# A decoder layer on one core: the expert's down projection written as two 64-token products per chunk

## The chip, the core and the metric

The kernel runs on one core of a Trainium2 chip. The core has five engines with a queue each: PE (TensorE, matrix products; the loading of its weights is listed apart as PEld), DVE (VectorE), ACT (ScalarE), POOL (GpSimd) and SP (SyncE, which here only issues transfers). PE reads its operands from SBUF and writes into PSUM[...]; DVE and ACT copy results out of it. The metric is the time of one execution on the device in microseconds, as the median of several runs. The profile is of one further execution.

## The reference, cut to what matters

One decoder layer with the normalisation after each part: causal self attention of 16 heads, linear cross attention to a context, then a mixture of experts with 8 experts of which each token uses two. There are 8 sequences of 112 tokens, so 896 tokens of 512 numbers. The change concerns the experts:

```python
gate_up = einsum('th,ehj->etj', h, gate_up_proj) + gate_up_proj_bias
gate = minimum(gate_up[..., ::2], 7);  up = clip(gate_up[..., 1::2], -7, 7)
act = (up + 1.0) * gate * sigmoid(1.702 * gate)
expert_out = einsum('eti,eih->eth', act, down_proj) + down_proj_bias
out = einsum('te,eth->th', scores, expert_out)
```

The inner size of an expert is 512, as is the size of a token. Everything is f32.

## The kernel before, in words

The layer is one stream of work. Up to about 755 us it does the two attentions, the routing, and the first product of the experts. From there on the experts' part has the core alone. Tokens have been sorted by expert into blocks of 128 in the DRAM tensor `store`, and the part is a loop over `STEPS` = 21 blocks, whatever the routing was.

For one block `s`:

- `fetch_tokens` (POOL, L944) brings the block's 128 tokens, `fetch_weights` (SP, L917 and L925) brings three matrices of 512x512 of the block's expert, `wg`, `wu` and `wd`, 1 MB each. They lie in 12 slabs of SBUF, three for each of the four blocks that can be ahead.
- `start` turns the tokens with four transposes on PE (`bT_ps`, L975), and ACT copies the result to SBUF (`bT`, L979).
- `project(s, st, k)` makes the gate (k = 0) and the up part (k = 1): four products over the chunks `c` of 128 of the contraction (L1054), summed in one PSUM bank, and then bias, limits and product on DVE and the sigmoid on ACT.
- `transposed_block` turns the activated block, again with four transposes on PE (`aT_ps`, L975) and a copy on ACT (`aT`, L979).
- `down(s, st)` is the down projection: four products over the chunks (L1080), with the stationary operand `aT[:, c, :]`, which is 128 rows of the contraction by 128 tokens, and the moving operand `wd[:, c, :]`, 128 rows by 512 columns. The result is 128 tokens by 512 in one bank, `yps`. ACT copies it to SBUF as `y` (L1091), and POOL adds it to the rows of `total` with an indirect DMA (L1094). In the last block, `finish` adds one more product into the same bank (L1198) and DVE reads it (L1199).

A product in f32 appears in the profile as two passes, each with its own weight load. So the four products of one `down` are eight matmul records and eight weight loads.

The order on PE, DVE, ACT and SP is that of the program text (`tc.manual_schedule`). In the loop over `s`, PE runs: gate product of block `s`, transposes of the activated block `s-1`, transposes of the tokens of block `s+1`, up product of block `s`, down product of block `s-1`. In the first blocks a few small products of the routing of the last tokens stand between these: `sTps` (L588, 8 columns of weights), `lps` (L515), `cps` (L540, L541) and `dbps` (L594, 8 rows of contraction). In the last ones `keys` (L1178) stands ahead of the down product. After the loop has reached its end, the last tokens are normalised (`close_steps`) and written to the output by POOL (`write`, L1129).

## Time and profile before

| | us |
|---|---|
| median of three runs (lowest, highest) | 1000.46 (999.9, 1000.54) |
| the profiled execution | 998.96 |
| its span, first to last instruction | 997.4 |
| PE busy | 963.8 |
| PE weight loads busy | 505.1 |
| DVE busy | 462.5 |
| ACT busy | 244.7 |
| POOL busy | 185.2 |
| matmuls of the down projection, 168 records, busy | 75.9 |
| mean granted clock of TensorE | 0.993 of full speed |

A matmul record lasts longer than its place in the stream[...]. So the mean of a record (595 ns for the down projection) isn't its cost; the distance from one start to the next is, or the busy time of the group divided by its count. In the chain of work that ended last the pieces are laid end to end, so that a piece's length is the time it took from the path.

### The profile page before, as it was taken

To read this page: it belongs to the slowest core of one execution; us is meant where nothing else is said; L and a number is where in the kernel's file an instruction comes from. 1 tells how busy PE (TensorE), PEld (TensorE's weight loads), DVE (VectorE), ACT (ScalarE), POOL (GpSimd) and SP (SyncE) were. 2 spreads that over 40 slices of the span, in tenths; PEclk is the share of its full clock that TensorE was granted. 3 is DMA by queue.
4 is the path that set the end of the run, shared out by engine and by line. 5 is a ranking of instruction groups with operands and counts; after the bars stand their busy time and mean duration, and the time that the engine had idled before them with its cause. 6 is when DMAs were issued, how large, how long until landed. Compare 5 with 4: busy or idle time off the path is not lost.

```text
span 997.4 us, 9419 instructions
## 1 busy us (share of the span) xinstructions
PE 963.8 (97%) x3271; PEld 505.1 (51%) x3271; DVE 462.5 (46%) x1036; ACT 244.7 (25%) x430; POOL 185.2 (19%) x235
## 2 busy tenths in 40 slices
PE   7998999999999999999999999999899999999994
PEld 3455544566446555654555455555454444444442
DVE  1356511154213542574414566567775533334384
ACT  1132311133103311322222222333124211121132
POOL 3133200033001414020002222211101212111132
PEclk9999999999999999999999999999999999999998
DMA  9990004111010001131001010110489997692333
GB/s 337 367 342 26 1 1 168 43 42 44 0 46 39 1 1 43 43 104 31 1 0 31 9 50 36 53 63 32 151 346 370 328 391 218 202 344 46 95 86 82
DMA packets 33839, 114.99 MB, mean 115 GB/s; under 512 B 3845, under 2 KB 8005, under 8 KB 26240
## 3 DMA queue, kind: packets, MB, share of 16 engines
q1 hardware_dynamic: 26784, 98.28, 26.9%
q0 software_dynamic: 6336, 15.75, 6.6%
q8 instruction: 26, 0.43, 0.2%
q10 hardware_dynamic: 672, 0.36, 0.1%
q14 instruction: 21, 0.17, 0.1%
HBM read 115.83 MB, written 29.01 MB: 145 GB/s over the span
## 4 chain that ended last, share of the span: by engine, by line
PE 86%; DVE 7%; issue 3%; ACT 1%; POOL 1%; DMA 1%; SPq 0%; POOLq 0%; DVEq 0%; ACTq 0%
PE gups L1054 13%; PE ops L237 10%; PE yps L1080 6%; PE vps L327 6%; PE zps L435 3%; PE xqps L870 2%; PE xgps L870 2%; PE sumps L812 2%; PE sps L387 2%; PE xops L237 2%; DVE z L843 1%; PE pps L427 1%; PE aT_ps L975 1%; PE bT_ps L975 1%; DVE p L412 1%
## 5 line engine op out<-in xcount | busy, mean ns | idle before, releaser
L1054 PE MATMUL gups<-slab,bT 128*128 128x512 f32 x336 | 151.5, 593 | 2.0 <-ACT bT L979 2.0
L1054 PEld LDWEIGHTS gups<-slab,bT 128*128 128x128 f32 x336 | 61.9, 190 | 71.4 <-issue 68.4
L237 PE MATMUL ops<-slab,zT 128*128 128x512 f32 x224 | 97.9, 592 | 0.0
L1062 DVE TENSOR_TENSOR gu<-gups,biases 128x512 f32<-128x512 f32 x42 | 29.0, 691 | 114.8 <-PE gups L1054 114.8
L1080 PE MATMUL yps<-slab,aT 128*128 128x512 f32 x168 | 75.9, 595 | 2.3 <-ACT aT L979 2.3
L237 PEld LDWEIGHTS ops<-slab,zT 128*128 128x128 f32 x224 | 42.0, 190 | 50.3 <-issue 49.5
L275 POOL TENSOR_TENSOR ws<-slab 128x256 f32<-128x256 f32 x16 | 11.8, 739 | 282.0 <-PE qk_5c L291 83.0
L327 PE MATMUL vps<-slab,x0T 128*112 128x512 f32 x128 | 58.6, 612 | 1.0 <-DVE x0T L187 0.8
L1094 POOL DMA_INDIRECT total<-y,nums x19 | 30.4, 1602 | 134.6 <-ACT y L1091 61.2
L1080 PEld LDWEIGHTS yps<-slab,aT 128*128 128x128 f32 x168 | 31.2, 190 | 40.6 <-issue 37.1
L244 DVE TENSOR_TENSOR xn<-xn,ops 128x512 f32<-128x512 f32 x28 | 19.2, 685 | 55.3 <-PE ops L237 55.2
L435 PEld LDWEIGHTS zps<-pT,v 112*128 112x128 f32 x256 | 33.5, 192 | 12.3 <-issue 11.2
L327 PEld LDWEIGHTS vps<-slab,x0T 128*112 128x112 f32 x128 | 22.8, 183 | 31.3 <-issue 29.7
L442 DVE COPY zT<-zps 128x448 f32<-128x448 f32 x32 | 20.0, 624 | 39.8 <-PE zps L435 39.8
L411 DVE TENSOR_REDUCE nm<-p 112x4 f32<-112x448 f32 x32 | 19.7, 616 | 30.9 <-POOL p L401 30.9
L435 PE MATMUL zps<-pT,v 112*128 112x112 f32 x256 | 33.4, 273 | 0.0
L1091 ACT COPY y<-yps 128x512 f32<-128x512 f32 x20 | 11.7, 584 | 87.8 <-issue 79.8
L237 PE MATMUL xops<-slab,gate 128*128 128x512 f32 x56 | 27.3, 632 | 3.8 <-DVE gate L845 2.6
L1066 ACT ACTIVATE sg<-gu 128x512 f32<-128x512 f32 x21 | 13.2, 630 | 71.2 <-DVE gu L1064 53.6
L565 POOL DMA_INDIRECT store<-xn,rows x14 | 13.9, 992 | 81.3 <-DVE count L627 52.5
L395 ACT ACTIVATE p<-sps 112x448 f32<-112x448 f32 x32 | 17.4, 544 | 45.6 <-PE sps L387 45.6
L387 PE MATMUL sps<-k,q 128*112 128x112 f32 x256 | 28.0, 262 | 0.0
(799 smaller groups left out, 1649.4 us busy)
## 6 DMA issues: line engine op xcount, KB each, us to landing
slab<-in_wg_dram SPq DMA_DIRECT2D x21, 1024.0 KB
slab<-in_wu_dram SPq DMA_DIRECT2D x21, 1024.0 KB
slab<-in_wd_dram SPq DMA_DIRECT2D x21, 1024.0 KB
store<-slab SPq DMA_DIRECT2D x8, 1806.0 KB
biases<-gubs SPq DMA_DIRECT2D x21, 512.0 KB
cT<-in_ctxT_dram SPq DMA_DIRECT2D x8, 750.0 KB
xblk<-store POOLq DMA_DIRECT2D x21, 258.0 KB, 7.4
slab<-in_wq_dram SPq DMA_DIRECT2D x4, 1024.0 KB
```

What stands on the lines that cost most here:

```text
L237: nc.tensor.matmul(ps, aT[:, c, t * P : (t + 1) * P], w[:, c, :], start=(c == 0), stop=(c == C - 1),)
L327: nc.tensor.matmul(ps[:S, :], xT[:, c, b * S : (b + 1) * S], w[:, c, :], start=(c == 0), stop=(c == C - 1),)
L387: nc.tensor.matmul(ps[:S, i * S : (i + 1) * S], qk["q"][:, rows], qk["k"][:, rows], start=True, stop=True,)
L435: nc.tensor.matmul(zps[:, i * S : (i + 1) * S], v[:, half * 4 + i, hl * DH : (hl + 1) * DH], pT[:, i * S : (i + 1) * S], start=True, stop= ...
L442: nc.vector.tensor_copy(zT[:, hl, half * HALF : (half + 1) * HALF], zps[:, :HALF])
L812: nc.tensor.matmul(sums[:, j, :], kf[:, sc, g * P : (g + 1) * P], vs[:, sc, g, :], start=(sc == 0), stop=(sc == NSC - 1),)
L870: nc.tensor.matmul(ps[:, :HALF], w[:, c, g * P : (g + 1) * P], xT[:, c, cols], start=(c == 0), stop=(c == C - 1),)
L975: nc.tensor.transpose(ps[:, c * P : (c + 1) * P], src[:, c * P : (c + 1) * P], ident)
L1054: nc.tensor.matmul(ps, st["bT"][:, c, :], st["w"][k][:, c, :], start=(c == 0), stop=(c == C - 1),)
L1062: nc.vector.tensor_add(a, ps, st["bias"][:, k * I : (k + 1) * I])
L1080: nc.tensor.matmul(ps, st["aT"][:, c, :], st["wd"][:, c, :], start=(c == 0), stop=(c == C - 1 and s < STEPS - 1),)
L1094: put = nc.gpsimd.indirect_dma_start(out=total, out_offset=bass.IndirectOffsetOnAxis(ap=st["num"], axis=0), in_=y, in_offset=None, compute ...
```

## The change

Each of the four products of `down` becomes two: one for the tokens 0 to 63, into partitions 0 to 63 of the bank, and one for the tokens 64 to 127, into partitions 64 to 127. Both have the same moving operand. The stationary operand of each is 64 columns wide, so the built program gives the first the tile of 128 rows by 64 columns of the array at column 0, and the second that at column 64. All other products of the loop keep the tile of 128 by 128. The order in `down` is, for each chunk: both passes of the first half, and then both passes of the second half. Nothing else is changed, and no other engine has an instruction more or less, or in another place.

```diff
         def down(s: int, st):
             ps = bank(f"yps_{s}", "aux")
             for c in range(C):
-                nc.tensor.matmul(
-                    ps,
-                    st["aT"][:, c, :],
-                    st["wd"][:, c, :],
-                    start=(c == 0),
-                    stop=(c == C - 1 and s < STEPS - 1),
-                )
+                for rows in (slice(0, P // 2), slice(P // 2, P)):
+                    nc.tensor.matmul(
+                        ps[rows],
+                        st["aT"][:, c, rows],
+                        st["wd"][:, c, :],
+                        start=(c == 0),
+                        stop=(c == C - 1 and s < STEPS - 1),
+                    )
```

## The prediction

> **What bounds the kernel now.** I read the first lines of the page, then the chain of work that ended last, since a busy share doesn't say whether an engine sets the end. The page's shares and its chain:

> ```profile
> PE 963.8 (97%) x3271; PEld 505.1 (51%) x3271; DVE 462.5 (46%) x1036; ACT 244.7 (25%) x430; POOL 185.2 (19%) x235
> ...
> PE 86%; DVE 7%; issue 3%; ACT 1%; POOL 1%; DMA 1%; SPq 0%; POOLq 0%; DVEq 0%; ACTq 0%
> ...
> L1080 PE MATMUL yps<-slab,aT 128*128 128x512 f32 x168 | 75.9, 595 | 2.3 <-ACT aT L979 2.3
> L1080 PEld LDWEIGHTS yps<-slab,aT 128*128 128x128 f32 x168 | 31.2, 190 | 40.6 <-issue 37.1
> ```

> PE is the bound, and the down projection has 75.9 us of it, with 2.3 us of waiting before it in the whole run. Then the same chain in order of time, from 755 us on. Columns: start, length (both us), engine and group, number of passes:

> ```profile
> 783.99 3.44 PE yps L1080 x8
> 787.42 0.32 PE sTps L588 x2
> 787.74 3.63 PE gups L1054 x8
> ...
> 795.67 1.05 PE dbps L594 x2
> 796.73 3.63 PE yps L1080 x8
> 800.36 3.43 PE gups L1054 x8
> ...
> 908.68 3.43 PE yps L1080 x8
> ...
> 942.43 0.22 PE keys L1178 x2
> ```

> From 755 to 965 us the chain holds PE alone, without a gap. A down projection is 3.43 us for 8 passes, so a pass of 512 columns costs 0.429 us. Whatever is added to PE there is added to the end.

> The groups that are longer than their work are the only places where the trace shows the array in another tile. `keys` and `sTps` are two passes of 128 columns each; `keys` takes 0.22, `sTps`, whose weights are 8 columns wide, takes 0.32, and the eight gate passes after it 3.63 where 3.43 is usual. `dbps` has 8 rows; it takes 1.05 where two passes are 0.86, and the group after it again 3.63. So going into another tile costs 0.10 (8 weight columns) to 0.19 us (128 columns), coming back 0.20. The weight loads in order of time say why:

> ```profile
> 786.40 0.19 PEld L1080 LDWEIGHTS yps<-slab,aT 128*128 128x128 f32 x1 [0.24 <-issue]
> 787.35 0.10 PEld L588 LDWEIGHTS sTps<-ident,sco 128*8 128x8 f32 x2 [0.76 <-DVE gu L1073]
> 787.66 0.30 PEld L1054 LDWEIGHTS gups<-slab,bT 128*128 128x128 f32 x2 [0.22 <-issue]
> ```

> Loads come every 0.43 us, each at the start of the pass before its own. The load for `sTps` comes 0.95 after its predecessor (0.43 + 0.52): it isn't made ahead. The same holds on the way back.

> [...] the first pass after a switch is recorded with 697 ns instead of 592, 105 more, and the difference between 0.19 and 0.10 is some 0.09 us for 120 columns.

> **The change, part by part.** It removes 8 passes per block and adds 16, each of 512 columns. The width of the weights isn't in the price of a pass: the 8-column passes of `sTps` still took 0.11 us each for 128 moving columns, as those of `keys` did. So by work alone PE has 16 × 0.429 = 6.86 us per block instead of 3.43. What saves it is only that the two halves run side by side; at best they come back to what one product does already. Nothing is there to gain from the shorter loads, as loads are hidden now (passes are 0.429 apart with loads of 0.19).

> *The order matters.* Call the halves A and B, and their passes 1 and 2. The stream is A1 A2 B1 B2 for each chunk. [...] So the pairs that overlap are A2 with B1, and B2 with the next chunk's A1. With l for the time that a 64-column load shows, 105 × 64/128 = 0.053 us (estimate from the recorded 697 − 592):

> - In this trace each load starts when the pass before its own starts, never sooner. Then B1's load begins with A2, and B1 runs l later. A1 at 0, A2 at 0.429, B1 at 0.482, B2 at 0.911, next A1 at 0.964. The last B2 starts at 3 × 0.964 + 0.911 = 3.803 and ends at 4.232. Against 3.432: **+0.80 us per block**.
> - If the load for an idle tile is made sooner[...]: **+0.46**.
> - If the halves do not overlap: 16 × 0.429 = 6.864: **+3.43**.

> I take the first, because it is the way this trace loads its weights.

> *The switches.* Each `down` now goes into the 64-column mode and back. In: 0.10 + 56 columns × 0.0008 = 0.146; back: 0.20 (3.63 − 3.43). Together **+0.343 per block**. Bounds: 0 (the one 64-column product now there, the bias transpose `gubps`, shows no gap, but it is a transpose) to 0.39 (0.19 + 0.20). Two `sTps` follow a `down` and two `dbps` stand before one; there a switch is paid already: −2 × 0.197 − 2 × 0.191 = −0.78 in all.

> *Which blocks are on the path.* The first 19 downs lie in the gapless part or directly behind it (965.3 to 968.7, with PE running on to 976). The 20th, at 976.0, is followed by a wait: PE stands idle for 2.27 us before the last, until ACT has copied `aT` at 981.81, and ACT itself is busy from 981.14 with a root that waits for DVE. The 20th's `y` copy starts at 981.35 though its passes end near 979.6, and the transposes end near 980.2. So some 1.5 us of delay are absorbed there. The last is on the path (its result goes through `finish`, DVE and POOL's write), but PE is drained when it starts, so the way in is free and a shorter load shows: 0.80 + 0.20 − 0.05 = 0.95.

> *What else could move.* No other engine gets an instruction. ACT's `y` copy and POOL's add come later with their block; they wait for PE already, by several us each (POOL 61.2 us in ten waits for `y`). SP's reload of the `wd` slab waits for the down product to end (the SP queue waited 92.5 us in all for it), but the weights of four blocks are ahead, and a slower loop asks for fewer bytes per us. The tile pool and semaphores are unchanged in kind. These I cost at nothing; the cover is the length of a block, 11.2 us.

> *The sum.* 19 × (0.80 + 0.343) − 0.78 + 0.95 = 21.9 us. On the profiled execution's 998.96 that makes 1020.9. The median of the runs is 1.5 us above that execution, so 1022.4.

> **The rivals.**

> *Side by side with loads made sooner.* 19 × 0.803 − 0.78 + 0.61 = 15.0: 1015.5. [...] Against it: here no load passes a pass that hasn't started. Without any switch cost, 20 × 0.457 = 9.1: 1009.6, the floor of this family.

> *One after the other.* 19 × 3.775 − 0.78 + (3.775 − 1.5) + 3.58 = 76.8: 1077.3. For it: nothing in the trace shows two passes at work at once[...]. Against it: [...]the built program places the halves on different columns.

> *Faster.* The one mechanism would be that an f32 pass streams at twice the rate in a 64-column tile[...]. Then the last pass would end at 2.315, which is 1.12 less than 3.43; less the switches that is −0.77 a block over 20 blocks, 985. It decides from about 0.34 us a pass down. Against it: `sTps`, in a column tile, streams its 128 columns no faster than `keys`.

> *Nothing changes* would need full overlap and free switches[...].

> **How the numbers follow.** Side by side with loads as now: 0.42, 1022.4, its own range 1018 to 1027 (switches 0.25 to 0.39, load 0.03 to 0.11). Side by side with early loads: 0.20, 1009 to 1017. One after the other: 0.30, 1074 to 1081. Faster 0.04, nothing within 0.2% 0.03, the rest 0.01. 0.2% is about 2 us, what a measurement of this kernel can tell. Serial work can't be left out of an 8-in-10 range, so it reaches from 1012 to 1080. Chances: faster 0.04, same 0.03, slower 0.93.

> **What would show it.** In the profile after: 16 passes per block at L1081; a chain piece of about 4.2 us for `yps` (3.9 with early loads, 6.9 serial); the start of B1 some 0.05 us after that of A2, with the next start 0.43 later, and not 0.43 between all sixteen; the first load of `yps` and the first `gups` load after it not made ahead, with that `gups` group at 3.63. Right total and wrong steps would be a `gups` of 3.43 with longer passes. The prediction is wrong if the passes of the two tiles are 0.43 apart, or if they are shorter than 0.43.

## The result, and the profile after

The changed kernel takes 1005.88 us as the median of three runs (1005.74 to 1006.33), against 1000.46 before: a ratio of 1.0058 with a 95% interval of 1.004 to 1.0076. Timed a second time it was 1005.83 us against 999.69, ratio 1.0059 (1.0046 to 1.0073). So it is slower, as forecast, but by 5.4 to 6.1 us and not by 22, and below the range that was given (1012 to 1080).

The profiled execution took 1005.74 us, its span is 1004.2. Its page, the lines that answer to those shown of before:

```profile
PE 970.4 (97%) x3439; PEld 495.8 (49%) x3439; DVE 462.8 (46%) x1036; ACT 244.9 (24%) x430; POOL 186.2 (19%) x235
...
L1081 PE MATMUL yps<-slab,aT 128*64 128x512 f32 x336 | 76.7, 599 | 2.1 <-ACT aT L979 2.1
...
L1081 PEld LDWEIGHTS yps<-slab,aT 128*64 128x64 f32 x336 | 22.3, 136 | 50.4 <-issue 46.0
```

Twice as many passes of the same 512 columns, 336 for 168, and 76.7 us busy for 75.9. The halves do run side by side: 16 passes in 3.58 us, where one pass of before is 0.429. The chain of work that ended last, in order of time (start, length, engine and group, passes):

```profile
785.06 3.58 PE yps L1081 x16
788.64 0.32 PE sTps L588 x2
788.96 3.63 PE gups L1054 x8
...
796.90 1.05 PE dbps L594 x2
797.95 3.58 PE yps L1081 x16
801.53 3.63 PE gups L1054 x8
```

A down projection is 3.58 us instead of 3.43, and the gate product behind it 3.63 instead of 3.43 in every block now, not only behind a `dbps` or `sTps`. That is the whole difference from the first down projection on, 5.9 of the 6.8 us between the two traces; the other 0.9 us lie ahead of it. The weight loads of one down projection in order of time show how the passes stand:

```profile
890.07 0.20 PEld L1081 LDWEIGHTS yps<-slab,aT 128*64 128x64 f32 x4 [0.76 <-issue]
890.55 0.14 PEld L1081 LDWEIGHTS yps<-slab,aT 128*64 128x64 f32 x2 [0.28 <-issue]
890.98 0.14 PEld L1081 LDWEIGHTS yps<-slab,aT 128*64 128x64 f32 x2 [0.29 <-issue]
891.41 0.14 PEld L1081 LDWEIGHTS yps<-slab,aT 128*64 128x64 f32 x2 [0.29 <-issue]
...
893.65 0.19 PEld L1054 LDWEIGHTS gups<-slab,bT 128*128 128x128 f32 x1 [0.81 <-issue]
```

The loads come two by two, one pair every 0.43 us, after four at the start. The starts of the matmuls in the same trace are 6 to 7 ns apart within a pair, and 0.48 us (the first) or 0.43 us from pair to pair: 8 places for 16 passes. (A record gives the shape of its tile but not which of the two tiles it is; which pass a start belongs to is inferred, here and in the experiments, from such counts.) The first load of `yps` comes 0.76 us after the load before it had ended, and the first of `gups` 0.81 us after: neither is made ahead. One block is 11.524 us from down to down, against 11.176 before, 0.348 more.

The part of the program ahead of the experts, which the change doesn't touch, differs between traces: the first gate product of the experts starts at 737.1 us before, 737.9 after and between 735.4 and 740.5 in the experiments. Most of it goes with the granted clock. In the clock record of the traces it falls to half for 3.4 us at a time: ahead of that gate product twice before (from 615.5 and from 721.3 us) and twice after (from 551.5 and from 677.8), never where it starts at 735.4, four times where it starts at 740.5, so about 0.9 to 1.3 us each (an estimate from these starts, as (737.1 − 735.4) / 2 and (740.5 − 735.4) / 4). From there to the last down projection the clock is whole in every trace. So the readings below rest on the pieces of the chain and the starts within the experts' part, and the medians only confirm them.

### The profile page after: what moved, and what is told of

The parts are those of the page before. It is cut to its first block, busy times and chain, and to the rows that moved or that the text cites. A ratio compares the mean times of both kernels' runs of the same rounds, so it can differ in the third digit from the quotient of the medians.

```text
span 1004.2 us, 9766 instructions
## 1 busy us (share of the span) xinstructions
PE 970.4 (97%) x3439; PEld 495.8 (49%) x3439; DVE 462.8 (46%) x1036; ACT 244.9 (24%) x430; POOL 186.2 (19%) x235
## 4 chain that ended last, share of the span: by engine, by line
PE 87%; DVE 7%; issue 2%; ACT 1%; POOL 1%; DMA 0%; POOLq 0%; DVEq 0%; ACTq 0%
PE gups L1054 14%; PE ops L237 10%; PE yps L1081 7%; PE vps L327 6%; PE zps L435 3%; PE xqps L870 2%; PE xgps L870 2%; PE sumps L812 2%; PE sps L387 2%; PE xops L237 2%; DVE z L843 1%; PE pps L427 1%; PE aT_ps L975 1%; PE bT_ps L975 1%; DVE p L412 1%
## 5 line engine op out<-in xcount | busy, mean ns | idle before, releaser
L1054 PE MATMUL gups<-slab,bT 128*128 128x512 f32 x336 | 153.2, 599 | 2.0 <-ACT bT L979 2.0
L1054 PEld LDWEIGHTS gups<-slab,bT 128*128 128x128 f32 x336 | 60.5, 190 | 77.1 <-issue 73.5
L1081 PE MATMUL yps<-slab,aT 128*64 128x512 f32 x336 | 76.7, 599 | 2.1 <-ACT aT L979 2.1
L1081 PEld LDWEIGHTS yps<-slab,aT 128*64 128x64 f32 x336 | 22.3, 136 | 50.4 <-issue 46.0
L435 PEld LDWEIGHTS zps<-pT,v 112*128 112x128 f32 x256 | 33.5, 192 | 12.3 <-issue 11.2
```

The costliest lines, as they stand in the source:

```text
L435: nc.tensor.matmul(zps[:, i * S : (i + 1) * S], v[:, half * 4 + i, hl * DH : (hl + 1) * DH], pT[:, i * S : (i + 1) * S], start=True, stop= ...
L1054: nc.tensor.matmul(ps, st["bT"][:, c, :], st["w"][k][:, c, :], start=(c == 0), stop=(c == C - 1),)
L1081: nc.tensor.matmul(ps[rows], st["aT"][:, c, rows], st["wd"][:, c, :], start=(c == 0), stop=(c == C - 1 and s < STEPS - 1),)
```

## The experiments

The pairs contradict the prediction, which had the program order A1 A2 B1 B2 (A and B the halves, 1 and 2 the two passes of an f32 product) pair A2 with B1. Theory A: each tile takes the next pass meant for it, past passes that wait for a busy tile, so that the pairs are A1 with B1 and A2 with B2; what is paid is only the switch of tiles. Theory B: passes start strictly in order, and the pairs are something else, the two passes of one product on one tile. Theory C: only products of different tiles that are neighbours overlap.

**All chunks of a half in a row.**

```diff
-            for c in range(C):
-                for rows in (slice(0, P // 2), slice(P // 2, P)):
+            for rows in (slice(0, P // 2), slice(P // 2, P)):
+                for c in range(C):
```

> The two loops of the down projection change places: all four chunks of the tokens 0 to 63 first, then all four of the tokens 64 to 127. The profile of the changed kernel shows its 16 passes in pairs that start 7 ns apart. Theory A, each tile takes the next pass that is meant for it, past passes that wait for another tile: if it looks far enough ahead (8 passes and 8 loads here), the pairs stay and the time is that of the changed kernel, about 1006 us, with 3.58 us of down projection per block. If it doesn't look so far, the first half has no partner at first and the block lies between 3.6 and 7.0 us. Theory B, passes start strictly in program order and what pairs up are the two passes of one product: pairs stay too, 1006 us. Theory C, only neighbouring products of different tiles overlap: one pair at the border, 15 places of 0.43 us, 6.6 us per block, about 1066 us.

Measured: 1041.64 us, ratio 1.042 (1.0391 to 1.0449). The chain and the loads of a down projection:

```profile
909.48 5.35 PE yps L1081 x16
914.83 3.63 PE gups L1054 x8
```

```profile
896.11 0.19 PEld L1081 LDWEIGHTS yps<-slab,aT 128*64 128x64 f32 x2 [0.76 <-issue]
896.60 0.14 PEld L1081 LDWEIGHTS yps<-slab,aT 128*64 128x64 f32 x1 [0.29 <-issue]
897.03 0.14 PEld L1081 LDWEIGHTS yps<-slab,aT 128*64 128x64 f32 x1 [0.29 <-issue]
897.46 0.14 PEld L1081 LDWEIGHTS yps<-slab,aT 128*64 128x64 f32 x1 [0.29 <-issue]
897.88 0.19 PEld L1081 LDWEIGHTS yps<-slab,aT 128*64 128x64 f32 x3 [0.29 <-issue]
898.31 0.19 PEld L1081 LDWEIGHTS yps<-slab,aT 128*64 128x64 f32 x2 [0.24 <-issue]
898.74 0.19 PEld L1081 LDWEIGHTS yps<-slab,aT 128*64 128x64 f32 x2 [0.24 <-issue]
899.23 0.14 PEld L1081 LDWEIGHTS yps<-slab,aT 128*64 128x64 f32 x1 [0.29 <-issue]
```

Loads come singly, until at 897.88, beside the fifth pass, a second stream sets in; then pairs; then single again. It is 12 places instead of 8 or 15: four passes of A alone, four of A with four of B, four of B alone. That is theory A with a limit. B1 stands behind all eight passes of A in the program. It starts when A5 does, when three of A's passes (A6, A7, A8) still wait ahead of it, and not sooner, with four or more. The next three passes of B start 0.057 us after their partners, not 0.006. Theory B wanted 8 places, theory C 15, and so does program order pass by pass; all fall here.

**The second half for one chunk only.**

```diff
                 for rows in (slice(0, P // 2), slice(P // 2, P)):
+                    if rows.start and c:
+                        continue
...
-                        stop=(c == C - 1 and s < STEPS - 1),
+                        stop=((rows.start or c == C - 1) and s < STEPS - 1),
```

> The second half of the tokens gets only its first chunk of the contraction (three quarters of its work are left out), so a down projection has 8 passes on the first tile and 2 on the second, 10 in all. Theory A, a pair is one pass of each tile: the first tile still needs 8 places of 0.43 us, two of them with a partner, 3.58 us per block, about 1006 us, and six single passes 0.43 apart in the profile. Theory B, a pair is the two passes of one product on one tile: 5 pairs, 2.3 us per block, about 980 us.

This leaves out three quarters of the second half's work. Measured: 1007.64 us, a single run. The chain:

```profile
913.50 3.58 PE yps L1083 x10
917.07 3.63 PE gups L1054 x8
```

Ten passes take what sixteen took. The starts are 7, 473, 7, 422, 429, 430, 429, 429 and 429 ns apart: two pairs, and then six single passes. The first tile sets the time with its eight passes and the second rides along, as A says; in strict order the very first pass would stand alone. Theory B's five pairs (2.3 us) are out. From the first down to the 19th the trace takes 212.22 us, the changed kernel's 212.34; what its one time is above the changed kernel's comes from the last down projection, which began at half the clock (passes 0.85 us apart).

**Gate and up in halves, down whole; and all three in halves.** In `project` the product over the chunks is written in halves in the same way, once on the kernel before and once on the changed one:

```diff
             for c in range(C):
-                nc.tensor.matmul(
-                    ps,
-                    st["bT"][:, c, :],
+                for rows in (slice(0, P // 2), slice(P // 2, P)):
+                    nc.tensor.matmul(
+                        ps[rows],
+                        st["bT"][:, c, rows],
...
```

> The gate and the up products are written in halves as the down product was, the down product is whole as before. The transposes stand between gate and up, so a block goes into the 64-column tiles twice and back twice. If a way in and back costs 0.15 + 0.20 us and halves themselves nothing, a block is 0.69 us longer than in the kernel before, 20 to 21 blocks, about 1014 us. If the cost goes with the number of split products, it is also twice that of the changed kernel, 1012 to 1014: only the run with all three in halves tells these apart.

> All three products of a block in halves. Down of a block and gate of the next but one stand side by side, so there is only one way in (before the up product) and one back (before the transposes) per block, with three times as many split passes as in the changed kernel. If only switches cost: as the changed kernel, 1006 us. If each split product costs 0.27 us as in the changed kernel's total: about 1017 us. If halves paired badly somewhere: gate or up groups longer than 3.6 us.

Measured: 1012.55 us for gate and up, ratio 1.0128 (1.0098 to 1.0157); 1009.04 us for all three, 1.0092 (1.0066 to 1.0119). One block of the chain with gate and up in halves:

```profile
902.41 0.59 PE aT_ps L975 x4
903.00 0.44 PE bT_ps L975 x4
903.43 3.58 PE gups L1055 x16
907.02 3.63 PE yps L1081 x8
910.65 3.59 PE gups L1055 x16
```

and one with all three:

```profile
911.72 0.59 PE aT_ps L975 x4
912.31 0.44 PE bT_ps L975 x4
912.75 3.58 PE gups L1055 x16
916.33 3.43 PE yps L1082 x16
919.76 3.43 PE gups L1055 x16
```

With all three in halves, only the first group behind the transposes is longer (3.58), and the transposes behind the last (0.59 for 0.44). Down and gate in halves, behind another product in halves, take 3.43, what they take whole. With gate and up in halves there are two ways in and two back: 3.58, 3.63, 3.59, 0.59. Per block, from the starts, it is 11.82 us and 11.47, against 11.18 before: +0.65 for two switches there and back, +0.30 for one. So the cost goes with the switches and not with the number of split products. All three in halves is still 3 us over the 1006 that I expected. In its last four blocks `keys` stands between up and down, in the whole tile, and brings an extra switch there and back; I hadn't counted that, nor the same around `sTps` and `dbps` in the first blocks. From the first down to the 19th its trace is 1.2 us longer than the changed kernel's. The profiled execution was the slowest of its four, 1011.62 us; of the rest of its distance, 2.9 us lie ahead of the first down, where the clock was halved four times and not twice, and 1.7 us behind the start of the last one, during which it was halved once more.

**Four products of 32 tokens.**

```diff
-                for rows in (slice(0, P // 2), slice(P // 2, P)):
+                for rows in (slice(i * P // 4, (i + 1) * P // 4) for i in range(4)):
```

> Four products of 32 tokens per chunk instead of two of 64. If the tiles take their passes independently, four run side by side, the block keeps its 8 places of 0.43 us, and only the way in gets shorter, by the load of 32 columns less (0.027 us): 0.5 us less than the changed kernel in all, 1005 to 1006 us. If it looks ahead too short a way for the fourth tile (its first pass stands behind three waiting passes), some places are 0.03 to 0.43 us longer and the down projection takes 3.7 to 7 us instead of 3.58.

Measured: 1006.12 us, ratio 1.0061 (1.0044 to 1.0078). The chain:

```profile
784.63 3.57 PE yps L1081 x32
788.20 0.20 PE sTps L588 x2
788.40 3.63 PE gups L1054 x8
...
797.39 3.57 PE yps L1081 x32
```

32 passes in 8 places, four at a time, 6 or 7 ns apart. The second place is 0.453 us behind the first instead of 0.480, 0.027 less, as estimated for 32 columns less of load. And `sTps` behind it, with 8 columns of weights, takes 0.20 instead of 0.32, no more than its two passes alone (0.11 each): behind passes of 32 columns this trace shows no way into `sTps`, which I had not planned. From the first down to the 19th it is 211.87 us for 212.34, the 0.5 us less that was expected. The median doesn't show it; in this trace the last down projection began at half the clock, and from its start to the end it is 1.6 us more than in the changed kernel's.

**Two chunks of a half in a row.**

```diff
-            for c in range(C):
-                for rows in (slice(0, P // 2), slice(P // 2, P)):
-                    nc.tensor.matmul(
+            for c, rows in (
+                (c, slice(h, h + P // 2))
+                for two in (0, 2)
+                for h in (0, P // 2)
+                for c in (two, two + 1)
+            ):
+                nc.tensor.matmul(
...
```

> Order of the products in a down projection: first half of the tokens for chunks 0 and 1, second half for chunks 0 and 1, and the same for chunks 2 and 3. In the run with all four chunks of a half in a row, the second half's first pass began as soon as it had three waiting passes ahead of it (beside the fifth of the first half), and the three after that 0.057 us late each. If that distance is the rule, here the second half starts beside the very first pass, and the down projection takes 3.6 to 4.0 us, some 0 to 8 us above the changed kernel in all. If what decided was something else (the fifth pass, the third chunk), the second half starts later, and it takes 4.5 us or more, over 1024 us.

Measured: 1004.12 us, a single run. The chain:

```profile
911.27 3.63 PE yps L1085 x16
914.90 3.63 PE gups L1054 x8
```

8 places again: B1, with three waiting passes of A ahead, starts 14 ns after A1. The last three partners come 0.057 us late, as before. So what counts is how much waits ahead, and not which chunk it is: three passes at most as far as these two orders show, or, counted in products, one that hasn't begun; they don't tell these apart.

The two orders also settle a milder form of program order that the list of theories lacked: that a product, with its two passes as a unit, may not start before the product ahead of it in the program. The changed kernel's 8 places would agree with it. But it would give 14 places for the first of these orders and 10 for this one, and they took 12 and 8. (That this one time is below the changed kernel's comes from the part ahead of the experts, where the clock was not halved: its first gate product starts at 735.4 us, 2.6 us sooner than in the changed kernel's trace. In the experts it is 0.05 us a block longer.)

**The kernel before without its own switches.** If a switch costs 0.3 to 0.4 us, those around `sTps` and `dbps` can go:

```diff
-    db = const.tile([E, D], F32, name="db")
-    nc.scalar.dma_start(out=db, in_=t_in["db"])
+    db = const.tile([P, D], F32, name="db")
+    nc.vector.memset(db, 0.0)
+    nc.scalar.dma_start(out=db[:E, :], in_=t_in["db"])
+    scores_T = [const.tile([P, P], F32, name=f"scores_T{i}") for i in range(2)]
+    for sT in scores_T:
+        nc.vector.memset(sT, 0.0)
...
-        nc.tensor.matmul(sps[:E, :P], sco, ident, start=True, stop=True)
-        sT = small.tile([E, P], F32, tag="sT", name=f"sT_{t}", bufs=2)
-        nc.scalar.copy(sT, sps[:E, :P])
+        nc.tensor.transpose(sps[:E, :P], sco, ident)
+        sT = scores_T[t % 2]
+        nc.scalar.copy(sT[:E, :], sps[:E, :P])
```

> The kernel before, without the change, and without its own switches of the tile: the scores are turned by a transpose (one pass; the bias transpose of 64 columns showed no gap around it) instead of a product with the identity, and the product with the biases of the down projection gets its 8 rows padded with zeros to 128. If a switch costs what the traces show (0.10 and 0.20 us around the score product, 0.19 and 0.19 around the bias product, seven of each) and PE is the bound there, 4.8 us go, and 0.8 us for seven passes less: about 995 us. If the wait around these is not the tile's but that of a small operand or of a late input, the time stays at 1000 us.

Measured: 997.78 us against 999.69, ratio 0.998 (0.997 to 0.9991): faster than both kernels, though by 1.9 us and not by 5. The chain:

```profile
783.81 3.43 PE yps L1084 x8
787.25 0.11 PE sTps L592
787.36 3.44 PE gups L1058 x8
...
795.10 0.86 PE dbps L598 x2
795.96 3.43 PE yps L1084 x8
```

Where PE bounds, everything that was promised is there: 0.11 for 0.32 (of which 0.11 is the pass that the transpose saves), 3.44 for 3.63, 0.86 for 1.05, 3.43 for 3.63; from the first to the 19th down 205.29 us for 206.87. That is two of the seven of each kind. The other five lie in the cross attention. There nothing seems to be gained: from the first `sumps` to the first gate product it is 205.6 us in the trace of before (531.59 to 737.15) and 205.5 in this one. The busy time of the engines in that stretch, of before and then of this kernel (length, then busy time and instructions of each engine):

```profile
531.00:740.00 209.00, 201.00 (x769) 111.28 (x768) 133.77 (x320) 58.54 (x95) 38.15 (x50) 0.98 0.23 84
```

```profile
531.00:740.00 209.00, 199.18 (x764) 112.70 (x763) 133.94 (x319) 58.67 (x95) 39.32 (x50) 0.98 0.24 88
```

PE has 1.8 us less to do in the same time. But the clock wasn't the same: it was halved for 3.4 us three times in this trace, all of them after 718 us, and twice in that of before. The end of the stretch in the trace of the two-chunk order, whose clock was not halved, in that of before, and in this one (the third number from the right is the granted clock):

```profile
718.00:737.00 19.00, 14.27 (x78) 9.47 (x77) 14.67 (x31) 5.28 (x8) 0.39 (x1) 1.00 1.01 406
718.00:737.00 19.00, 14.27 (x74) 9.29 (x72) 13.17 (x31) 5.28 (x8) 0.00 (x0) 0.91 1.01 403
718.00:737.00 19.00, 15.43 (x67) 10.87 (x68) 10.29 (x30) 4.70 (x7) 0.00 (x0) 0.73 1.01 406
```

So the kernels are to be compared where both ran at the full clock. From the first group of `sumps` to the seventh, at about 702 us, this kernel takes 169.85 us; the two-chunk order and the run with one chunk of the second half, which have the program of before up to there, take 171.31 and 171.37. Here 1.5 us are gained, and the slower clock hides them afterwards. It is about half of the 2.8 us that were promised for the four `sTps` and three `dbps` up to there: PE was idle for 8 us in the stretch already, so others set part of the time, and my "PE is the bound there" held in full only from 755 us on. With the 1.6 us in the experts this makes 3.1, and runs with the same mean clock of 0.992 differ by as much: 998.0 us on average (ten runs) for 1001.0 (two runs of before). Why this kernel had that lower clock in ten of its twelve runs, and the one before mostly 0.993, isn't shown.

## Why the prediction was right or wrong

**That it is slower, and why:** right. The switch of tiles is on the path in every block and nothing pays for it. *In 0.146, back 0.20*: measured 0.15 and 0.20 (3.58 − 3.43 and 3.63 − 3.43), 0.348 per block for 0.343. *The −0.78 for switches that were there already*: from the first down to the 19th the changed trace is 212.34 us for 206.87, 5.47 more; 18 × 0.348 less 0.78 is 5.48.

**That the two halves run side by side on their tiles:** right, though no trace of before showed it: it was my estimate. The rival of serial work is out by the 8 places.

**The pairs of A2 with B1: this is the step that failed**, and all of the difference. They need starts in program order, which no trace of before showed: it was my estimate. The step gave +0.80 us per block, or +0.46 with early loads, of which 0.43 is a ninth place of 0.429 and the rest an allowance for starts that wasn't shown either. The runs put it at nothing for this order: the two tiles take their passes independently, up to three waiting ones ahead, so A1 goes with B1 and A2 with B2, 6 to 7 ns apart. With starts in order the sixteen passes of the changed kernel need nine places and those of the first experiment 15; they took 8 and 12, and the order of whole products fails too (14 and 10 places for the 12 and 8 of the two reordered experiments).

**"Each load starts when the pass before its own starts, never sooner":** true of before, where the passes of the large products all had the whole tile and loads came every 0.43 us, and no ground for the case of two. I took a regularity of one tile as a rule for both, and so preferred +0.80 to +0.46; neither was it. The 0.05 us of a shown load is real, but it is paid once per down projection, at the first place (0.480 for 0.429, and 0.453 with 32 columns), as part of the way in. The 0.057 us of the late partners in the two reordered experiments are about as long; that they are a load as well isn't shown.

**Which blocks are on the path:** right. Between the starts of the 19th and the 20th down it is 0.34 us more; between the 20th and the last nothing (6.38 for 6.41, and 6.48 in the second trace of the changed kernel), absorbed ahead of ACT's copy of `aT` as said (PE waits 2.14 us for it before the last, 2.27 in the trace of before); from the last to the end 0.15, the 0.20 of the way back less the 0.05 of the shorter load.

**The sum** without the failed term, 19 × 0.343 − 0.78 + 0.15, is 5.9 us, which is what was measured (5.4 and 6.1). **The range** missed because both of my cases of overlap held the same wrong assumption on the order. A case with the halves in step and only the switches to pay, 1006, wasn't in the list, and "no change" had a chance of 0.03. Apart from this, the limit given for the faster rival, 0.34 us a pass, leaves the switches out: with them 9 passes + 7 × 0.053 + 0.343 = 3.43 gives 0.30.

## What to carry to other kernels

Ask of a change to array tiles two things apart: whether the tiles run side by side, and how often the tile size changes along PE's queue. Here the first cost nothing with tiles of 64 or of 32 columns (8 places of 0.43 us with either), and a change there and back cost 0.30 to 0.35 us wherever PE was the bound. Small products with few rows or few columns between large ones paid it unseen (0.10 and 0.20 us at `sTps`, 0.19 and 0.20 at `dbps`): padding one to the full tile, and writing the other, a product with the identity, as a transpose, took the switches away.

Splitting the stationary columns of a product that already had the tile of 128 by 128 gained nothing here: with one, two or four tiles a down projection is 8 places of 0.43 us, and each pass still has all 512 moving columns.

Before a small gain in a stretch is denied, look at the granted clock of both traces there: two times of 205.5 and 205.6 us hid a gain of 1.5.
